# Twelve pairs of layer-1 row gathers made early and parked in DRAM, in a two-layer graph attention kernel

## The chip, the cores and the metric

The kernel runs on one core of a Trainium2 chip. The metric is the device time of one execution in microseconds (us). A core has five engines that run their own instruction streams: PE (TensorE, matmuls), DVE (VectorE), ACT (ScalarE), POOL (GpSimd) and SP (which only issues DMAs here). POOL also issues the indirect DMAs, which gather rows of a table by a list of row numbers.

## What is computed

A graph of N = 6250 nodes and E = 100000 edges, sorted by target, plus one own edge per node. Node features x are normalised, and then pass two graph attention layers and a small dense network:

```python
h = relu(layernorm(x))                        # (6250, 768)
# gat_conv(h, src, dst, W, a_src, a_dst, b, heads), with 4 heads in layer 1 and 1 head in layer 2:
h = (h @ W).reshape(n, heads, -1)             # 256 columns in all
alpha_s = (h * a_src).sum(-1); alpha_d = (h * a_dst).sum(-1)
e = leaky_relu(alpha_s[src] + alpha_d[dst], 0.2)
e = exp(e - segment_max(e, dst)[dst])
alpha = e / segment_sum(e, dst)[dst]
out = segment_sum(h[src] * alpha, dst) + b
# relu after each layer; then
out = x + relu(h @ Wm1 + bm1) @ Wm2 + bm2     # (6250, 768)
```

## The kernel before

All sizes go by 128 partitions. The nodes are NT = 49 tiles of 128, the edges 782 tiles of 128. Four edge tiles are a group (NG = 196 groups), two are a pair, and the work of four groups stands beside one node tile. Three stages follow one another.

**The feature stage** (loop over the 49 node tiles, after L386). SP loads a tile of x and its transpose. DVE takes the moments and subtracts the means (`centre`, L339), ACT applies relu (L341), PE multiplies by W1 in six fp32 products (`features1`, L350), and ACT writes the 256 results into the tile's row block in SBUF, `kept[i]` (`keep1`, L356), where each head has a column of ones beside its 64 columns. The eight scores of a node (source and target, four heads) are sums over products of its row with `a1`: POOL makes the products and adds halves (L365, L368), for the last four tiles DVE makes the products (L375), DVE adds the rest (L377), and ACT copies the four source scores to the end of the row (L378). `store1` (L381) then sends the row block to `table[1]` in DRAM.

**The edge stage of each layer** (`layer_edges`, L530) starts when the table is whole. POOL issues one indirect DMA for each edge tile (`gather`, L554), which brings the 128 source rows of 264 (layer 2: 258) numbers into one half of a pair buffer `G`. There are 20 pair buffers, and the gathers of group g + 8 are placed beside the work of group g (`AHEAD`). For each pair (`pair`, L612), ACT takes two exponentials of the source scores (L619, L621), DVE multiplies the second with the target's factor (L624), takes the maximum with the first (L634, in layer 2 L627), and weights the rows with it (L636; in layer 2 L631 puts the weight into the one-hot matrix instead). PE then adds the weighted rows to their targets, with a one-hot matrix of the targets ("hot", L582) as the other operand (L648). Masks for the target factors are made by DVE in layer 1 (L571), sent to DRAM, and read back in layer 2. When a node tile's sums are whole (`gather_up`, L659), its last steps are put on a list, and `advance` (L687) lets each of them go one step further, twice a group: `Node1.steps` (L796) divides, transposes, multiplies by W2, and stores the row block to `table[2]`, resting in between for a number of such half-groups (`rest`, L510). Layer 2's steps are the dense network and the output.

**Early gathers.** To bridge the wait for the last table rows, the first edge tiles of each layer are gathered before the table is whole (`EARLY`, L48). A row number that lies beyond the rows already stored is set to 0 and marked (`first_places`, L278); the missing rows are added later: DVE compares the source numbers with the numbers of the missing node tiles (`first_hits`, L258), PE multiplies the result with the `kept` tiles (`first_whole`, L273), and DVE joins both (L275). Layer 1 has 8 such gathers (L300): four once node tiles 0 to 43 are stored and four once 0 to 45 are. Layer 2 has 11: two behind tiles 0 to 45 and nine behind 0 to 46.

The order on each engine is the order in which the program is written; nothing reorders it. The engines wait for one another by semaphores.

Of the kernel before, what the change touches and what calls it, by code (L numbers as in the profile page):

```python
# [46 lines left out]

EARLY = {1: ((4, NT - 5), (4, NT - 3)), 2: ((2, NT - 3), (9, NT - 2))}  # L48
THERE = {layer: [there for n, there in stages for _ in range(n)] for layer, stages in EARLY.items()}

@with_exitstack
def kernel(
# [52 lines left out]

    iota_ps = ps.tile([P, P], F32, name="iota_ps", bufs=1)
    nc.vector.tensor_copy(iota_ps, iota)
    eps_c = const.tile([P, 1], F32, name="eps_c")  # L110
    nc.vector.memset(eps_c, EPS)
# [77 lines left out]
    def edge_places(ones):  # L189

        dst_i = ones.tile([P, NET], I32, name="dst_i")
        dri = ones.tile([NCH, CH], I32, name="dri")
        for to, of in ((dst_i, dst_cols), (dri, dst_rows), (src_i, src_cols)):
            nc.sync.dma_start(to, of)
            yield
            yield
        for layer in bT:
            with nc.allow_non_contiguous_dma(reason="256 numbers"):
                nc.sync.dma_start(bT[layer], {1: b1, 2: b2}[layer].rearrange("(k p) -> p k", p=P))
            yield  # L200
        b = ones.tile([P, OUT_DIM // P], F32, name="b")
        with nc.allow_non_contiguous_dma(reason="768 numbers"):
            nc.sync.dma_start(b, bm2.rearrange("(p k) -> p k", p=P))
        yield

        drm = ones.tile([NCH, CH], BF16, name="drm")
        nc.scalar.activation(dst_f, dst_i, AF.Copy)
        yield
        for d, to in ((dst_i, dcol), (dri, drm)):
            nc.vector.tensor_scalar(d, d, PAD_DST | P - 1, None, ALU.bitwise_and)  # L210
            yield
            nc.scalar.activation(to, d, AF.Copy)
            yield
        nc.sync.dma_start(dmod_d, drm)
        bp = ones.tile([P, 3, OUT_DIM // P], BF16, name="bp")
        rest = ones.tile([P, 2, OUT_DIM // P], F32, name="brest")
        in_parts(nc.vector, [bp[:, k] for k in range(3)], b, rest[:, 0], rest[:, 1])
        yield
        with nc.allow_non_contiguous_dma(reason="768 numbers"):
            nc.sync.dma_start(bm2_d.rearrange("s (p k) -> p s k", p=P), bp)  # L220
# [41 lines left out]
    def first_whole(pool, layer):  # L262

        j = 0
        for stage, (n, there) in enumerate(EARLY[layer]):
            if stage and layer == 1:
                first_hits(pool, layer, stage)
            for k in range(n):
# [23 lines left out]
    def first_rows(layer, stage):  # L292

        j = sum(n for n, _ in EARLY[layer][:stage])
        n, there = EARLY[layer][stage]
        for j in range(j, j + n):
            k, t = divmod(FIRST + j, 2)
            if k not in first_G[layer]:
                first_G[layer][k] = rows_in(layer)
            nc.gpsimd.indirect_dma_start(  # L300
                out=first_G[layer][k][:, t], out_offset=None, in_=table[layer][:there * P],
                in_offset=bass.IndirectOffsetOnAxis(ap=first_i[layer][:, j:j + 1], axis=0))
    mask_d = dram.tile([NU * P, 8 * P], BF16, name="mask_d")
    edges_stack.enter_context(tc.manual_schedule())
    with tc.tile_pool(name="w1p", bufs=1) as wp, tc.tile_pool(name="x1", bufs=6) as xp, \
# [38 lines left out]
        def features1(i):  # L344
            r, rstd = rs.pop(i)
            h_ps = ps.tile([P, HID], F32, name="h_ps", tag="o", bufs=3)
            for k in range(KI):
                if (i, k) == (1, 2):
                    spread_means(2)
                nc.tensor.matmul(h_ps, r[:, k], w1[:, k], start=(k == 0), stop=(k == KI - 1))  # L350
            return h_ps, rstd

        def keep1(i, h_ps, rstd):
            row = kept[i]
            h = heads_row(row)[:, :, :HID // 4]
            nc.scalar.activation(h, h_ps.rearrange("p (h c) -> p h c", h=4), AF.Copy, scale=rstd)  # L356

            ha = wk.tile([P, 8, HID // 4], F32, name="ha", bufs=2)
            four = ha.rearrange("p (k h) c -> p k h c", k=2)
            of = h.unsqueeze(1).to_broadcast([P, 2, 4, HID // 4])  # L360
            if i >= NT - 4:
                halves[i] = four, of
                return
            else:
                nc.gpsimd.tensor_tensor(four, of, a1b, ALU.mult)  # L365
                for n in (HID // 8, HID // 16):
                    hb = wk.tile([P, 8, n], F32, name=f"ha{n}", bufs=2 if n > 16 else 4)
                    nc.gpsimd.tensor_tensor(hb, ha[:, :, :n], ha[:, :, n:], ALU.add)  # L368
                    ha = hb
            halves[i] = ha  # L370

        def scores1(i):
            if i >= NT - 4:
                four, of = halves[i]
                nc.vector.tensor_tensor(four, of, a1b, ALU.mult)  # L375
                halves[i] = four.rearrange("p k h c -> p (k h) c")
            nc.vector.tensor_reduce(sd[1][:, i], halves.pop(i), AX.X, ALU.add)  # L377
# [18 lines left out]
        fetch_x(1)  # L396
        w1 = wp.tile([P, KI, HID], F32, name="w1")
        nc.sync.dma_start(w1, W1.rearrange("(k p) f -> p k f", p=P))
        fetch_xT(1)
# [5 lines left out]
        fetch_x(5)  # L405
        pieces = edge_places(ones)
        moments(0)
        spread_means(0)
# [5 lines left out]
        for i in range(NT):  # L414
# [23 lines left out]
            if i == 40:  # L438
                first_places()
            if i < NT - 5:  # L440
                keep1(i, *h)
                if i > 2:
                    store1(i - 3)
                if i > 1:
                    scores1(i - 2)
            else:
                for k in {NT - 3: (i - 2, i - 1)}.get(i, (i - 2,) if i < NT - 3 else (i - 1,)):
                    scores1(k)
                    if k == NT - 7:
                        store1(k - 1)  # L450
                    store1(k)
                keep1(i, *h)
            if i == NT - 6:
                first_sources(1)
            if i == NT - 4:
                first_rows(1, 0)
            elif i == NT - 2:
                first_rows(1, 1)
            if i >= 14:
                next(pieces, None)  # L460

        scores1(NT - 1)
        store1(NT - 1)

# [65 lines left out]
    def layer_edges(layer, H, node, pre, matched, pre_pool):  # L530
# [4 lines left out]
        with tc.tile_pool(name=f"eg{layer}", bufs=5) as eg, \  # L535
                tc.tile_pool(name=f"hw{layer}", bufs=10 if layer == 1 else 14) as hwp, \
                tc.tile_pool(name=f"sum{layer}", bufs=4) as sums, \
                tc.tile_pool(name=f"sm{layer}", bufs=4) as sm:
            G, hot, e_ps, o_ps = {}, {}, {}, {}

# [4 lines left out]
            def gather(g):  # L545
                if not 0 <= g < NG:
                    return
                for t in tiles(g):
                    k = TPG * g + t
                    if k // 2 not in G:  # L550
                        G[k // 2] = first_G[layer].get(k // 2) or rows_in(layer)
                    if k < FIRST + len(THERE[layer]):
                        continue
# [58 lines left out]
            def pair(g, p):  # L612
# [10 lines left out]
                rho, v, w = (e_ps[g // 4][:, at:at + 2, k * H:(k + 1) * H] for k in range(3, 6))  # L623
                nc.vector.tensor_mul(v, e2, rho)  # L624
                if layer == 2:
                    w = sm.tile([P, 2, H], F32, name="w")
                    nc.vector.tensor_max(w, v, e1)  # L627
                    hw = hwp.tile([P, 2, P], F32, name="hw")
# [4 lines left out]
                else:  # L633
                    nc.vector.tensor_max(w, v, e1)  # L634
                    hw = hwp.tile([P, 2, H, C + 1], F32, name="hw")
# [58 lines left out]
            if layer == 1:  # L694
                for r in range(4):
                    fetch_rows(r)
                first_whole(pre_pool, layer)
                for u in range(4):
# [9 lines left out]
            for g in range(NG):  # L708
# [14 lines left out]
                if j == 0:  # L723
                    if layer == 1:
                        fetch_rows(t + 4)
                    node.prefetch(t)
                    meet(t + 1)
                elif j == (2 if t < NT - 1 else 1):
                    node.ahead(t)
                elif j % 2:  # L730
                    make_mask((g + 7) // 2)
                if g == NG - 3:
# [12 lines left out]
                if NG - 3 <= g < NG - 1:  # L745
                    stay_warm(3)
                hot.pop(g, None)
                if layer == 1 and g == NG - 6:
# [24 lines left out]
    with tc.tile_pool(name="w2p", bufs=1) as wp, tc.tile_pool(name="wk2", bufs=2) as wk:  # L773
# [4 lines left out]
        class Node1:  # L778
# [17 lines left out]
            def steps(self, t, sum_, most=None, last=None):  # L796
# [12 lines left out]
                turn(o, p)  # L809
                yield from rest(7)  # L810
                rT = straighten(wk, 1, p)
                h_ps = ps.tile([P, HID + 2], F32, name="h_ps", tag="n")
                for k in range(KH):
                    nc.tensor.matmul(h_ps, rT[:, k], w2[:, k], start=(k == 0), stop=(k == KH - 1))
                yield from rest(7)
                row = kept[t][:, :TW[2]]
# [5 lines left out]
        with tc.tile_pool(name="pre1", bufs=1) as pre:  # L822
            first_hits(pre, 1, 0)
            pre1 = prepare(pre, 1, 4)
# [430 lines left out]
```

## Time and profile before

| | |
|---|---|
| median of 12 executions | 2148.82 us (2144.61 to 2150.55) |
| the profiled execution | 2148.88 us, of which the span from first to last instruction is 2147.0 us |
| mean granted TensorE clock | 0.828 of full |
| feature stage | about 0 to 155 us |
| gathers of layer 1 on POOL | 147.3 to 1135.6 us |
| gathers of layer 2 on POOL | 1141.3 to 2120.4 us |

The profile lists for each engine the time in which it ran instructions. A group of instructions is shown with its source line, engine, operation, output and inputs, the number of times, the summed time, the mean of one in ns, and the idle time of the engine just before it with what ended most of that. A row of the timeline has start, length, engine, line, operation and, in brackets, the idle time before it and what ended it; "issue" means that nothing the profile shows was waited for. Time in which an engine issues a plain DMA isn't counted as busy, but the indirect DMAs on POOL are.

### The profile page before, as it was taken

Reading aid. Unit: us, or ns where it says so; the run is one execution under the profiler, and the core shown is the slowest. Engines: PE = TensorE matmul, PEld = TensorE weight load, DVE = VectorE, ACT = ScalarE, POOL = GpSimd, SP = SyncE. Lnnn points to the kernel's source line nnn. Section 1 sums busy time; section 2 is a strip of 40 time slices with the busy share of each in tenths; the row PEclk is TensorE's granted clock in tenths of the full one; section 3 lists DMA queues with packets and bytes.
Section 4 is the critical chain, followed back from the end, with each engine's and each line's share of the span. In section 5 each row is a group of like instructions: output and inputs, shape, how many; then the busy total and the mean of one; then the engine's idle time right before and its main releaser. Section 6 shows DMA issues by size and latency. Waiting matters only on the chain.

```text
span 2147.0 us, 26518 instructions
## 1 busy us (share of the span) xinstructions
PE 1580.6 (74%) x6764; PEld 1087.1 (51%) x6765; DVE 1345.6 (63%) x4164; ACT 597.3 (28%) x2601; POOL 1602.6 (75%) x1759
## 2 busy tenths in 40 slices
PE   8997766666676666666668677777787787787777
PEld 6875444444444444444446454554554454454554
DVE  7887776667666667666666555555555555555554
ACT  4651222222222222222222222222222222222222
POOL 6877777777777777777776777777777777777773
PEclk9998878777777778777879888888878878888898
DMA  9966565555555555655556455556556556555553
GB/s 347 363 223 215 172 168 165 168 168 164 169 167 162 169 167 162 171 166 160 163 141 208 125 172 179 164 171 180 169 167 180 176 159 180 179 156 179 180 153 112
DMA packets 157543, 383.12 MB, mean 178 GB/s; under 512 B 35543, under 2 KB 50222, under 8 KB 157382
## 3 DMA queue, kind: packets, MB, share of 16 engines
q0 software_dynamic: 75072, 209.10, 36.5%
q1 hardware_dynamic: 80940, 170.75, 22.6%
q10 hardware_dynamic: 1370, 1.48, 0.3%
q8 instruction: 58, 0.95, 0.2%
q14 instruction: 103, 0.84, 0.1%
HBM read 323.07 MB, written 58.13 MB: 178 GB/s over the span
## 4 chain that ended last, share of the span: by engine, by line
DMA 32%; PE 26%; DVE 20%; issue 9%; POOL 6%; ACT 6%; ACTq 0%; DVEq 0%; POOLq 0%
DMA G<-table,src_i 32%; PE o_ps L648 11%; PE y_ps L939 7%; POOL G L554 6%; DVE hw L636 5%; PE h_ps L350 5%; DVE e_ps L624 2%; ACT e L619 2%; DVE hw L631 2%; DVE e_ps L634 2%; DVE hot L582 2%; ACT sum L678 2%; DVE acc L669 1%; PE y_ps L875 1%; PE tp L923 1%
## 5 line engine op out<-in xcount | busy, mean ns | idle before, releaser
L554 POOL DMA_INDIRECT G<-table,src_i x1545 | 1472.0, 953 | 470.7 <-issue 260.8
L648 PE MATMUL o_ps<-hw,hot 128*128 128x260 f32 x1564 | 576.9, 516 | 310.7 <-DVE hw L636 300.5
L648 PE MATMUL o_ps<-G,hw 128*128 128x258 f32 x1564 | 473.1, 439 | 227.4 <-DVE hw L631 227.0
L648 PEld LDWEIGHTS o_ps<-hw,hot 128*128 128x128 f32 x1564 | 362.3, 251 | 486.8 <-DVE hw L636 412.5
L624 DVE TENSOR_TENSOR e_ps<-e,e_ps 128x8 f32<-128x8 f32 (+1 forms) x782 | 129.7, 166 | 676.1 <-ACT e L621 667.9
L648 PEld LDWEIGHTS o_ps<-G,hw 128*128 128x128 f32 x1564 | 318.9, 217 | 355.1 <-DVE hw L631 294.2
L619 ACT ACTIVATE e<-G 128x8 f32<-128x8 f32 (+1 forms) x782 | 160.2, 205 | 1063.4 <-DMA G<-table,src_i 1022.6
L631 DVE TENSOR_SCALAR hw<-iota_ps,dcol,w 128x128 f32<-128x128 f32 x782 | 285.0, 406 | 14.4
L636 DVE TENSOR_TENSOR hw<-G,e_ps 128x520 f32<-128x520 f32 x391 | 271.8, 695 | 14.3 <-DVE e_ps L634 0.9
L678 ACT ACTIVATE sum<-acc 32x260 f32<-32x260 f32 (+1 forms) x384 | 160.0, 417 | 332.0 <-DVE acc L669 321.2
L939 PE MATMUL y_ps<-wm,mT 128*128 128x384 f32 x392 | 205.4, 660 | 0.7 <-ACT mT L928 0.7
L621 ACT ACTIVATE e<-G 128x8 f32<-128x8 f32 (+1 forms) x782 | 148.8, 190 | 0.7
L350 PE MATMUL h_ps<-w,r 128*128 128x256 f32 x588 | 135.2, 384 | 4.4 <-ACT r L341 4.4
L582 DVE TENSOR_TENSOR hot<-iota_ps,dcol 128x512 f32<-128x512 f32 x196 | 133.7, 682 | 0.0
L939 PEld LDWEIGHTS y_ps<-wm,mT 128*128 128x128 f32 x392 | 87.7, 248 | 66.2 <-issue 40.4
L350 PEld LDWEIGHTS h_ps<-w,r 128*128 128x128 f32 x588 | 109.7, 193 | 22.7 <-ACT r L341 5.7
L669 DVE SCALAR_TENSOR_TENSOR acc<-acc,keep,o_ps 128x260 f32<-128x260 f32 (+1 forms) x192 | 91.4, 476 | 0.4 <-PE o_ps L648 0.4
L634 DVE TENSOR_TENSOR e_ps<-e_ps,e 128x8 f32<-128x8 f32 x391 | 68.2, 174 | 13.4
L365 POOL TENSOR_TENSOR ha<-kept,a1b 128x512 f32<-128x512 f32 x45 | 53.2, 1183 | 26.9 <-ACT kept L356 26.8
L627 DVE TENSOR_TENSOR w<-e_ps,e 128x2 f32<-128x2 f32 x391 | 62.4, 159 | 13.3
L600 PEld LDWEIGHTS <-mask 128*128 128x128 bf16 x1564 | 57.3, 100 | 15.2 <-issue 8.3
L769 ACT ACTIVATE rT<-tp,bT 128x128 f32<-128x128 f32 x196 | 59.4, 352 | 7.1 <-PE tp L763 7.1
(405 smaller groups left out, 1124.2 us busy)
## 6 DMA issues: line engine op xcount, KB each, us to landing
xt<-in_x SPq DMA_DIRECT2D x96, 384.0 KB, 5.2
drow<-dmod_d SPq DMA_DIRECT2D x49, 512.0 KB, 5.2
mask_d<-mask SPq DMA_DIRECT2D x97, 256.0 KB, 2.5
mask<-mask_d SPq DMA_DIRECT2D x97, 256.0 KB, 5.0
G<-table,src_i POOLq DMA_INDIRECT x1545, 2.9
xTt<-in_xT SPq DMA_DIRECT2D x49, 384.0 KB, 5.8
out<-y SPq DMA_DIRECT2D x48, 384.0 KB, 2.3
table<-kept SPq DMA_DIRECT2D x49, 132.0 KB, 4.0
```

The costliest lines, as they stand in the source:

```text
L350: nc.tensor.matmul(h_ps, r[:, k], w1[:, k], start=(k == 0), stop=(k == KI - 1))
L554: nc.gpsimd.indirect_dma_start(out=G[k // 2][:, k % 2], out_offset=None, in_=table[layer], in_offset=bass.IndirectOffsetOnAxis(ap=src_i[:, ...
L582: nc.vector.tensor_tensor(hot[g][:, T[0]:T[0] + n], iota_ps.unsqueeze(1).to_broadcast([P, n, P]), dcol[:, k:k + n].unsqueeze(2).to_broadca ...
L619: nc.scalar.activation(e1, sc, AF.Exp)
L621: nc.scalar.activation(e2, sc, AF.Exp, scale=SLOPE)
L624: nc.vector.tensor_mul(v, e2, rho)
L631: nc.vector.tensor_scalar(hw[:, t], iota_ps, dcol[:, k:k + 1], w[:, t], ALU.is_equal, ALU.mult)
L636: nc.vector.tensor_mul(hw, Gp[:, :, :RW[1]].rearrange("p t (h c) -> p t h c", h=H), w.unsqueeze(3).to_broadcast([P, 2, H, C + 1]))
L648: nc.tensor.matmul(o_ps[u], l, r[:, :RW[layer]], start=(g % 2 == 0 and k == 0), stop=(g % 2 == 1 and k == tiles(g)[-1]))
L669: nc.vector.scalar_tensor_tensor(acc, run[0], keep[:, u % 2:u % 2 + 1], o_ps.pop(u), ALU.mult, ALU.add)
L678: nc.scalar.activation(done[t][r], acc[r], AF.Copy)
L939: nc.tensor.matmul(y_ps, mT[:, j], wm2[:, j, s * half:(s + 1) * half], start=False, stop=(j == KH - 1))
```

## The change

Layer 1 has no early gathers of its first tiles any more. In their place 24 gathers of 12 later pairs (pairs 23, 39, 55 and so on to 199, one in every two node tiles' work) are made near the end of the feature stage, each once the rows up to a given node tile are stored: four after 38 tiles, two each after 39 to 44, four after 45, two each after 46 and 47. Their rows go to DRAM (`soon_away`, on SP) and come back into a pair buffer when the gather of that pair would have been due (`soon_back`, on SP). The missing rows, of 11 to 2 node tiles, are made by DVE compares (`soon_hits`), PE products (`soon_missing`) and a DVE joining step (`soon_whole`), spread over the work of node tiles 0 to 24: each node tile has the work of one edge tile. The compares read the node numbers from PSUM (`nid_ps`).

The scores become eight more columns of W1 from node tile 8 on: POOL multiplies W1 with `a1` at the start, DVE sums into the weight columns, PE multiplies 264 columns in place of 256, and ACT copies the scores out of the result twice (to the row and to `sd`). Tiles 0 to 7 have their scores made as before, during tiles 8 to 15. From node tile 35 on a row block is stored in its own step of the loop.

In `pair`, the weighting of a pair's rows and the products with them (`onto_sums`) move behind the first weight operation of the next pair, save in the last two groups of a layer. Both rests of `Node1.steps` go from 7 to 4.

```diff
-EARLY = {1: ((4, NT - 5), (4, NT - 3)), 2: ((2, NT - 3), (9, NT - 2))}
+EARLY = {2: ((2, NT - 3), (9, NT - 2))}
...
+SOON = [NT - m for m in (11, 11, 10, 9, 8, 7, 6, 5, 4, 4, 3, 2)]
+SOON_AT = {2 * (8 * i + 11) + 1: i for i in range(len(SOON))}
+BARE = 8
...
+    def soon_rows(there):
+        for i in range(len(SOON)):
+            if SOON[i] == there:
+                soon_G[i] = rows_in(1)
+                for t in range(2):
+                    nc.gpsimd.indirect_dma_start(
+                        out=soon_G[i][:, t], out_offset=None, in_=table[1][:there * P],
+                        in_offset=bass.IndirectOffsetOnAxis(ap=soon_i[:, i, t:t + 1], axis=0))
+    def soon_away():
+        for i in range(len(SOON)):
+            nc.sync.dma_start(soon_d[i], soon_G.pop(i).rearrange("p t c -> p (t c)"))
+    def soon_back(i):
+        G = rows_in(1)
+        nc.sync.dma_start(G.rearrange("p t c -> p (t c)"), soon_d[i])
+        return G
...
+    def soon_hits(pool, k):
+        i, t = divmod(k, 2)
+        if i < len(SOON):
+            m = NT - SOON[i]
+            soon_hit[k] = pool.tile([P, NT - SOON[0], P], F32, name="soon_hit")
+            nc.vector.tensor_tensor(
+                soon_hit[k][:, :m],
+                soon_of[i][:, t * P:(t + 1) * P].unsqueeze(1).to_broadcast([P, m, P]),
+                nid_ps[:, SOON[i]:].unsqueeze(2).to_broadcast([P, m, P]), ALU.is_equal)
+    def soon_missing(k):
+        if 0 <= k < 2 * len(SOON):
+            there, hit = SOON[k // 2], soon_hit.pop(k)
+            soon_p[k] = ps.tile([P, TW[1]], F32, name="missing1", tag="n")
+            for T in range(there, NT):
+                nc.tensor.matmul(soon_p[k], hit[:, T - there], kept[T], start=(T == there),
+                                 stop=(T == NT - 1))
+    def soon_whole(G, k):
+        if 0 <= k < 2 * len(SOON):
+            i, t = divmod(k, 2)
+            row = G[soon_pair[i]][:, t]
+            nc.vector.scalar_tensor_tensor(row, row, soon_ok[:, i, t:t + 1], soon_p.pop(k),
+                                           ALU.mult, ALU.add)
...
-                nc.tensor.matmul(h_ps, r[:, k], w1[:, k], start=(k == 0), stop=(k == KI - 1))
+                nc.tensor.matmul(h_ps[:, :n], r[:, k], w1[:, k, :n], start=(k == 0), stop=(k == KI - 1))
...
+            if i >= BARE:
+                nc.scalar.activation(row[:, RW[1]:], h_ps[:, HID:HID + 4], AF.Copy, scale=rstd)
+                nc.scalar.activation(sd[1][:, i], h_ps[:, HID:], AF.Copy, scale=rstd)
...
+            if BARE < i <= SOON[0] - 3:
+                store1(i - 1)
+            if i >= SOON[0] - 3:
+                store1(i)
+                soon_rows(i + 1)
...
                 nc.vector.tensor_mul(v, e2, rho)
+                while weighed:
+                    onto_sums(*weighed.pop())
...
+                weighed.append((g, p, Gp, w))
+                if g >= NG - 2:
+                    onto_sums(*weighed.pop())
...
-                first_whole(pre_pool, layer)
+                soon_sources(pre_pool, 0)
+                soon_away()
+                fetch_rows(3)
...
+                    if layer == 1:
+                        soon_hits(pre_pool, t)
                 elif j % 2:
+                    if layer == 1 and j == 3:
+                        soon_missing(t)
+                    elif layer == 1:
+                        soon_whole(G, t - 1)
...
-                yield from rest(7)
+                yield from rest(4)
```

## The prediction

> **What bounds the kernel now.** I read the busy rows of the page first, then GpSimd (POOL) in order of time, because one group of its instructions, the row gathers, fills it.
>
> ```profile
> PE 1580.6 (74%) x6764; PEld 1087.1 (51%) x6765; DVE 1345.6 (63%) x4164; ACT 597.3 (28%) x2601; POOL 1602.6 (75%) x1759
> L554 POOL DMA_INDIRECT G<-table,src_i x1545 | 1472.0, 953 | 470.7 <-issue 260.8
> L648 PE MATMUL o_ps<-hw,hot 128*128 128x260 f32 x1564 | 576.9, 516 | 310.7 <-DVE hw L636 300.5
> L582 DVE TENSOR_TENSOR hot<-iota_ps,dcol 128x512 f32<-128x512 f32 x196 | 133.7, 682 | 0.0
> ```
>
> No engine looks full. But the 470.7 us of idle time over 1545 gathers is 0.305 us each, and the timeline of POOL shows what that is:
>
> ```profile
> 143.11 1.18 POOL L365 TENSOR_TENSOR ha<-kept,a1b 128x512 f32<-128x512 f32 x1 [0.18 <-ACT kept L356]
> ...
> 147.31 1.13 POOL L300 DMA_INDIRECT G<-table,first_i  x1 [1.67 <-DMA table<-kept]
> ...
> 158.49 1.01 POOL L554 DMA_INDIRECT G<-table,src_i  x1 [0.37 <-issue]
> ...
> 213.17 1.18 POOL L554 DMA_INDIRECT G<-table,src_i  x1 [0.30 <-issue]
> ...
> 1134.64 0.94 POOL L554 DMA_INDIRECT G<-table,src_i  x1 [0.30 <-issue]
> 1141.26 0.95 POOL L300 DMA_INDIRECT G<-table,first_i  x1 [5.67 <-DMA table<-kept]
> ...
> 1155.39 0.95 POOL L554 DMA_INDIRECT G<-table,src_i  x1 [0.30 <-DVE G L275]
> ```
>
> Every gather is followed by 0.30 us in which POOL starts the next one, whoever is named as releaser. One gather is thus 0.95 + 0.30 = 1.25 us of POOL, and it runs so without a break, but for the 5.67 us between the layers, from 147.3 us to the last gather at 2119.4 us. After that 26.6 us of tail remain (2147.0 - 2120.4). The 774 gathers of layer 1 took 1135.6 - 158.5 = 977.1 us (1.262 each), the 771 of layer 2 965.0 us (1.252 each). ACT waits 1022.6 us in all for gathered rows. So the time is: when the gathers begin, plus how many there are, plus the gap between the layers, plus the tail. POOL time saved in the edge layers comes off the end one for one, while the other engines have room. Do they? The table by stretches:
>
> ```profile
> 200.00:220.00 20.00, 12.65 (x57) 8.21 (x55) 16.29 (x45) 4.31 (x29) 15.12 (x17) 0.91 0.55 163
> 600.00:700.00 100.00, 69.69 (x270) 46.56 (x268) 67.42 (x187) 24.66 (x118) 76.09 (x79) 0.76 0.57 164
> ```
>
> The columns are length, PE, PEld, DVE, ACT, POOL, clock, DMA share, GB/s. In steady state PE and DVE are two thirds busy. From 181 to 222 us the consumers catch up on rows that are already there: by 222.4 us, 8 + (222.4 - 158.5) / 1.262 = 59 gathers (14.7 groups of four) had been issued, and all were consumed in 41.8 us. That is 2.8 us a group, 11.4 us a node tile (four groups), where POOL needs 16 x 1.26 = 20.2.
>
> **Gathers moved ahead.** Layer 1 loses its 8 early gathers and gets 24 (12 pairs of edge tiles). The stream behind them falls from 774 to 758: 16 x 1.25 = 20.0 us less, if it starts when it did. The 24 stand on POOL in front of the stream, each behind a table store: 24 x 1.3 (the 8 early ones of before averaged 1.40, beside DVE work that goes away) = 31 us. The row of node tile i is kept at ACT L356; I read 119.3 us for tile 37, 142.6 for 44, 148.0 for 46, 153.3 for 48. A store lands a median 4.0 us after issue. The first four gathers can go at 119.3 + 0.5 + 0.3 + 4.0 = 124 us, four at tile 44's landing (147), two each at 45's and 46's. By these the soon gathers end near 157 to 158 and tile 48's row has landed by 153.3 + 0.5 + 0.4 + 4.0 = 158: both limits fall where the stream starts today. POOL's score products, 45 x about 2.5 us, which filled it here until 145.6 us, are gone from tile 8 on, so it has the room.
>
> **Scores as columns.** Each feature tile on PE grows from 256 to 264 columns:
>
> ```profile
> 139.77 2.76 PE L350 MATMUL h_ps<-w,r 128*128 128x256 f32 x12
> ```
>
> 2.76 / 256 x 8 = 0.086 us, over 41 tiles 3.5 us. In the feature stage PE runs back to back but for the stalls on loads (4.7 us in two steps at 130 to 137 us, DMA nearly full until about 120 us), and a later PE fits into those: I take 1.5 us, with bounds 0 and 3.5. The second small ACT copy (0.20) fits: ACT has 1.8 us of work in a 2.70 us tile. POOL's six weight products (15 us from 12.5 us on) end before DVE's reductions of tiles 2 to 4 and before tile 8 needs them. So the stream begins at 158.5 + 1.5 = 160.0 us. That tile 48 no longer waits for a score product on DVE (0.69 + 0.69 us) is within this.
>
> **The missing rows and the way through DRAM.** 12 x 270 KB out and back on SP. The nearest row, a mask of 256 KB, lands in 5.0 us; reads are issued eight groups (40 us) ahead of use. The copies out stand behind three row fetches and hold 12 of the 20 pair buffers; the first is needed again by the 17th gather of the stream, 20 us after its start, by which time the first copies have gone. Nothing on POOL waits. The stores of tiles 35 to 48 now wait on SP for their own tile's row; behind them are loads needed five tiles (13 us) later. On PE the missing rows take 160 products of 128x264. Twelve such took
>
> ```profile
> 171.72 5.75 PE L273 MATMUL missing<-kept,hit 128*128 128x264 f32 x24 [0.98 <-DVE hit L258]
> ```
>
> 0.48 us each at a high clock; an edge product at the layer's clock of 0.77 takes 576.9 / 782 = 0.74. In the first four tiles, 10 or 11 products are 5.3 to 8.1 us, beside 13.2 us of PE work in a steady tile and a POOL pace that is now 15 gathers, 18.8 us. PE can thus fall 0 to 2.5 us behind per tile. The Trainium skill ("TensorE: Matmul & The Clock Gate", section "Part 1: The HAM clock gate") says that the clock comes back after about 3.4 us of sustained activity, which favours the lower end; the rows agree in kind (granted 1.00 in the full feature stage, 0.77 here). By either, the sum over all 24 tiles is at most 17 us, and POOL may run 20 pairs, 50 us, ahead before it waits for a buffer. I take 0. DVE gets 160 x 128 elements of compare, by the L582 row (682 / 512 = 1.33 ns) 27 us, and 24 corrections of 0.49 = 12 us, over 450 us: 68% becomes 77%.
>
> Here a rule speaks against the change. The skill ("GPSIMD Engine Reference", section "8. Key points") has GpSimd share its SBUF interfaces with VectorE, with contention when a DVE instruction has two SBUF inputs or runs in a two-port mode. The trace has both sides:
>
> ```profile
> 213.05 0.48 DVE L571 TENSOR_SCALAR mask<-drow,pidx 128x1024 bf16<-128x1024 bf16 x1
> 181.66 0.68 DVE L582 TENSOR_TENSOR hot<-iota_ps,dcol 128x512 f32<-128x512 f32 x1
> 181.56 0.95 POOL L554 DMA_INDIRECT G<-table,src_i  x1 [0.30 <-issue]
> ```
>
> The gather beside the mask took 1.18, the one beside the "hot" compare, which has one operand in PSUM, 0.95. The new compares also have one operand in PSUM (nid_ps), and so have the corrections. By the nearest row, "hot", they cost POOL 0; if they held it for all their length, 27 + 12 = 39 us.
>
> **One slot later, and the shorter rests.** The weighted rows of a pair now wait on DVE behind the next pair's first weight product, which waits for that pair's rows. PE gets them 2.5 us later, and a pair buffer comes free one pair of 20 later; while POOL bounds, 0. At the end of each layer the last two groups go at once, so the tail stays. Bounds -1 to +2. The rest counts fall from 7 to 4 half-groups. Counting the steps, tile 45's row of table 2 leaves one group earlier (group 193, not 194), tile 46's at 194 in both. At the gap between the layers two gathers need tiles up to 45, nine need 46. The two move into the 5.67 us gap: 2 x 1.25 = 2.5 us gained (bounds 0 and 5).
>
> **Sum.** -20.0 (16 gathers) + 1.5 (start) - 2.5 (gap) = -21.0 us. The profiled execution took 2148.88 us (span 2147.0 + 1.9), level with the median of 2148.82. 2148.8 - 21 = 2128 us.
>
> **The rivals.** Within 0.2% is 4.3 us, about what a measurement of this kernel tells from no change.
> - As summed, with its bounds: 2122 to 2134. POOL's unbroken row speaks for it. Chance 0.80.
> - The stream starts later. If the two ACT copies, or slower loads beside the early gathers, lengthen feature tiles by 0.2 us on the path (41 x 0.2 = 8.2), the time is 2136; half of the idle 0.35 us that DVE shows ahead of "cent" in each tile speaks against it. Chance 0.09.
> - PE becomes the bound in the first tiles and the buffers don't absorb it: 2128 + 17 = 2145. The catching up at 2.8 us a group speaks against it. Chance 0.05.
> - Slower: the 24 compares and 24 corrections of node tiles 0 to 24 hold GpSimd's gathers. Held throughout, 2128 + 39 = 2167; it ends above 2153 from 25 / 39, two thirds of their length, on. The mask held a gather 0.2 of its 0.48 us, "hot" not at all. Chance 0.06.
>
> Faster by over 0.2%: 0.89; within: 0.05; slower: 0.06. The range 2122 to 2139 takes in the first two cases.
>
> **What would show it.** Right: the first gather of table 1 near 125 us, the stream's first at 159 to 162, 1.25 us each with no idle time but 0.30, layer 1's last gather near 1117, the gap between the layers about 3 us. Wrong: gathers over 1.1 us beside the new compares; POOL waiting on DVE or PE for a buffer in the first 200 us of the layer; feature tiles above 2.8 us.

## The result and the profile after

The changed kernel takes 2127.83 us in the median (2126.13 to 2132.72, 7 executions) beside 2148.45 us for the kernel before: ratio 0.991, 95% interval 0.9901 to 0.9919. That is 20.6 us less. The prediction was 2128 us. The sum came out right, but two of its terms did not. They were off by about as much in opposite directions, so that the total fits this closely is luck.

The page of the profiled execution (2130.58 us, of which the span is 2128.8 us) has these rows of engines and of the layer-1 and layer-2 gathers:

```profile
PE 1617.6 (76%) x7020; PEld 1128.2 (53%) x7021; DVE 1276.1 (60%) x4178; ACT 601.2 (28%) x2642; POOL 1527.2 (72%) x1666
L621 POOL DMA_INDIRECT G<-table,src_i x1529 | 1456.3, 952 | 467.8 <-issue 266.3
```

Sixteen gathers have gone from the streams (1529 for 1545). PE was busy 37 us longer: the products for missing rows (L366) take 90.2 us, while the edge products of layer 1 (L723) took 36 us less than in the kernel before (540.7 for 576.9).

```profile
L723 PE MATMUL o_ps<-hw,hot 128*128 128x260 f32 x1564 | 540.7, 490 | 242.7 <-DVE hw L711 241.3
L366 PE MATMUL missing<-kept,soon_hit 128*128 128x264 f32 x320 | 90.2, 441 | 0.0
```

DVE was busy 69 us less, and this comes with the deferral of the weighted rows: DVE was busy 1264.6 us in the kernel before with the deferral alone, and 1355.7 us in the changed kernel without it (both runs follow). DVE has no less to do, for its rows add up to about the same before and after (1427 and 1437 us); its instructions overlap more. The timeline of POOL in the changed kernel gives the places where the time went (start, length, operation, idle time before it):

```profile
126.13 1.13 POOL L331 DMA_INDIRECT G<-table,soon_i  x1 [79.78 <-DMA xt<-in_x]
...
155.06 0.95 POOL L331 DMA_INDIRECT G<-table,soon_i  x1 [0.30 <-issue]
156.31 0.95 POOL L621 DMA_INDIRECT G<-table,src_i  x1 [0.30 <-issue]
...
1111.04 0.95 POOL L621 DMA_INDIRECT G<-table,src_i  x1 [0.30 <-issue]
1112.30 0.94 POOL L309 DMA_INDIRECT G<-table,first_i  x1 [0.30 <-issue]
...
1117.00 0.94 POOL L309 DMA_INDIRECT G<-table,first_i  x1 [2.51 <-DVE e_ps L696]
...
1130.63 0.94 POOL L621 DMA_INDIRECT G<-table,src_i  x1 [2.31 <-DVE G L284]
...
2095.47 0.95 POOL L621 DMA_INDIRECT G<-table,src_i  x1 [0.30 <-issue]
```

The 24 early gathers run from 126.1 us to 156.0 us at 1.25 us each, and the stream follows with no gap. Set beside the kernel before (its rows are in the prediction), the span divides so:

| stretch of the span | before | after | difference |
|---|---|---|---|
| to the start of layer 1's stream | 158.49 | 156.31 | -2.2 |
| layer 1's stream (774 and 758 gathers) | 977.1 | 955.7 | -21.4 |
| its end to the start of layer 2's stream | 19.8 | 18.6 | -1.2 |
| layer 2's stream (771 gathers) | 965.0 | 965.8 | +0.8 |
| last gather to the end | 26.6 | 32.4 | +5.7 |
| span | 2147.0 | 2128.8 | -18.2 |

The profiled execution lies 2.8 us above the median of the timed ones. The gap between the layers and the end vary by some 3 us from profile to profile, also among kernels that are alike there, so single differences in these two rows are rough.

The windows show that PE and DVE took the extra work beside the gathers (columns as in the prediction). The first row is the kernel before, the other three are the changed kernel:

```profile
260.00:400.00 140.00, 93.93 (x398) 65.30 (x398) 96.56 (x270) 34.53 (x168) 105.95 (x112) 0.79 0.60 170
200.00:220.00 20.00, 15.24 (x72) 11.76 (x71) 15.25 (x40) 3.91 (x20) 15.12 (x17) 0.84 0.61 174
260.00:400.00 140.00, 115.04 (x552) 90.31 (x551) 109.99 (x297) 35.31 (x181) 106.12 (x112) 0.88 0.64 183
600.00:700.00 100.00, 72.83 (x290) 48.55 (x290) 70.09 (x199) 24.75 (x125) 75.93 (x80) 0.78 0.61 173
```

POOL's busy time per microsecond (the fifth pair) is the same in all of them, while PE rises from 67% to 82% where the missing rows are made, and DVE from 69% to 79%.

### The profile page after: what moved, and what is told of

Same layout as the page of the kernel before. It is cut to its first block, busy times and chain, and to the rows that moved or that the text cites. A ratio compares the mean times of both kernels' runs of the same rounds, so it can differ in the third digit from the quotient of the medians.

```text
span 2128.8 us, 27330 instructions
## 1 busy us (share of the span) xinstructions
PE 1617.6 (76%) x7020; PEld 1128.2 (53%) x7021; DVE 1276.1 (60%) x4178; ACT 601.2 (28%) x2642; POOL 1527.2 (72%) x1666
## 4 chain that ended last, share of the span: by engine, by line
DMA 32%; PE 27%; DVE 21%; issue 9%; POOL 6%; ACT 5%; ACTq 0%; DVEq 0%; SPq 0%; POOLq 0%
DMA G<-table,src_i 30%; PE o_ps L723 11%; DVE hw L711 8%; PE y_ps L1023 6%; PE h_ps L424 6%; POOL G L621 6%; DVE e_ps L691 2%; ACT e L686 2%; ACT sum L753 2%; DVE e_ps L696 2%; DVE hw L707 2%; DVE acc L744 1%; DVE mask L638 1%; DVE hot L649 1%; ACT e L688 1%
## 5 line engine op out<-in xcount | busy, mean ns | idle before, releaser
L621 POOL DMA_INDIRECT G<-table,src_i x1529 | 1456.3, 952 | 467.8 <-issue 266.3
L723 PE MATMUL o_ps<-hw,hot 128*128 128x260 f32 x1564 | 540.7, 490 | 242.7 <-DVE hw L711 241.3
L723 PE MATMUL o_ps<-G,hw 128*128 128x258 f32 x1564 | 467.6, 436 | 233.4 <-DVE hw L707 233.0
L723 PEld LDWEIGHTS o_ps<-hw,hot 128*128 128x128 f32 x1564 | 340.9, 235 | 402.0 <-DVE hw L711 348.2
L723 PEld LDWEIGHTS o_ps<-G,hw 128*128 128x128 f32 x1564 | 316.5, 215 | 358.8 <-DVE hw L707 288.2
L424 PE MATMUL h_ps<-w,r 128*128 128x264 f32 (+1 forms) x588 | 136.1, 386 | 1.5 <-ACT r L414 1.4
L366 PE MATMUL missing<-kept,soon_hit 128*128 128x264 f32 x320 | 90.2, 441 | 0.0
L331 POOL DMA_INDIRECT G<-table,soon_i x24 | 22.9, 953 | 86.8 <-DMA xt<-in_x 79.8
L366 PEld LDWEIGHTS missing<-kept,soon_hit 128*128 128x128 f32 x320 | 73.5, 230 | 16.8
```

The source lines that it names most:

```text
L366: nc.tensor.matmul(soon_p[k], hit[:, T - there], kept[T], start=(T == there), stop=(T == NT - 1))
L424: nc.tensor.matmul(h_ps[:, :n], r[:, k], w1[:, k, :n], start=(k == 0), stop=(k == KI - 1))
L621: nc.gpsimd.indirect_dma_start(out=G[k // 2][:, k % 2], out_offset=None, in_=table[layer], in_offset=bass.IndirectOffsetOnAxis(ap=src_i[:, ...
L723: nc.tensor.matmul(o_ps[u], l, r[:, :RW[layer]], start=(g % 2 == 0 and k == 0), stop=(g % 2 == 1 and k == tiles(g)[-1]))
```

## The experiments

Every run is given with its ratio to the kernel before on the same chip and the 95% interval, since the kernel before itself took 2148.2 to 2152.7 us on the chips used.

**No deferral.** The weighted rows follow their own weight again.

```diff
-                if g >= NG - 2:
+                if g >= 0:
                     onto_sums(*weighed.pop())
```

> The changed kernel with a pair's weighted rows and products again straight behind its own weight, everywhere. Theory (the deferral lengthens the end of layer 2: the products of group 193's second pair stand on PE behind two steps of the dense network, and the sum of the last but one 64 targets waits for them): the time from the last gather to the end falls from 32.4 us back to about 26.6, the second wait of POOL between the layers (2.31 us) shrinks or goes, and the whole takes 2120 to 2123 us. Rival (the longer end is a chance of the granted clock, and the deferral costs nothing, as the prediction had it): 2127 to 2129 us, with an end above 30 us in this profile too or below it in both.

Measured: 2122.97 us, 0.9881 (0.9867 to 0.9895); 4.9 us less than the changed kernel. From the last gather to the end it took 27.3 us in place of 32.4. The reason is in the order of DVE and PE near the end. DVE in the kernel before, where the partial sum of the last but one stretch of 64 targets (`acc`) comes straight after the weights:

```profile
2120.88 0.73 DVE L631 TENSOR_SCALAR hw<-iota_ps,dcol,w 128x128 f32<-128x128 f32 x2
2121.53 0.48 DVE L669 SCALAR_TENSOR_TENSOR acc<-acc,keep,o_ps 128x258 f32<-128x258 f32 x1
```

PE and then DVE in the changed kernel:

```profile
2097.60 2.63 PE L1023 MATMUL y_ps<-wm,mT 128*128 128x384 f32 x4
2100.16 0.33 PE L959 MATMUL y_ps<-bm2r,ones_r 3*128 3x384 bf16 x1
2100.43 1.56 PE L1023 MATMUL y_ps<-wm,mT 128*128 128x384 f32 x4
...
2102.89 0.48 DVE L744 SCALAR_TENSOR_TENSOR acc<-acc,keep,o_ps 128x258 f32<-128x258 f32 x1 [3.68 <-PE o_ps L723]
```

DVE in this run:

```profile
2098.68 0.47 DVE L744 SCALAR_TENSOR_TENSOR acc<-acc,keep,o_ps 128x258 f32<-128x258 f32 x1
```

The last gather started at 2119.40 us before and at 2095.47 after. Counted from there, `acc` comes after 2.1 us and after 7.4 us. With the deferral the products of group 193's second pair stand on PE behind two halves of a dense layer (the `y_ps` rows, 4.8 us with their bias products). Without it, `acc` is at 2098.68 us, 2.8 us after the last gather's start at 2095.91. From `acc` to the end of the span it is 25.5 us before, 25.9 us in the changed kernel and 25.5 us in this run, so the later `acc` is nearly the whole of the longer end. POOL's second wait between the layers was 1.60 us for 2.31. Layer 1's stream (956.5 us) and layer 2's (964.9) are the same with and without deferral, within 1 us: the deferral does nothing for the steady stretch, as the prediction had it, and costs at the end, as it had not.

**Deferral up to group 192.** `NG - 3` in place of `NG - 2` in the same line.

> The changed kernel with the deferral kept up to group 192 and the immediate order from group 193 on (three last groups in place of two). Theory (only the second pair of group 193 matters): as without any deferral, an end of about 26.6 us and 2120 to 2123 us. If deferring costs or gives something in the steady stretch as well, this run and the one without any deferral differ by more than 1.5 us. Rival (deferral without effect): 2127 to 2129 us.

Measured: 2125.53 us, 0.9893 (0.9879 to 0.9908). The end took 26.9 us in the profile, so the deferral in group 193 is what lengthens it. The timed median is above the 2120 to 2123 us that I had named, and 2.6 us above that without any deferral, more than the 1.5 us named beforehand, but the intervals overlap. The profile has the difference between the layers: 20.1 us there, 17.8 without deferral. Whether deferral also costs there is not settled by these two runs.

**Only the deferral, in the kernel before.** The same lines of `pair`, nothing else.

> The kernel before with nothing but the deferral of a pair's weighted rows (as in the changed kernel, save in the last two groups of a layer). Theory (the deferral gives nothing while the gathers bound the layers, and costs 3 to 6 us at the end of layer 2): the last gather at 2120 us as before, an end of 29 to 32.5 us in place of 26.65, and 0.1 to 0.3% more than the kernel before (2150.5 to 2155 where that takes 2148.5). Rival (the deferral costs nothing): the ratio is 1.000.

Measured: 2151.67 us, 1.002 (1.0011 to 1.0029), 3.5 us slower than the kernel before. The end took 32.1 us for 26.65. In this profile POOL also waited 8.63 us between the layers (5.67 before); the span, 2157.5, lies well above the median, so only the end is read from it. By itself this part of the change is a loss.

The profiles of this document fall into two groups. In the seven with the deferral in group 193, `acc` comes 6.0 to 8.2 us after the start of the last gather, and the end takes 29.1 to 32.4 us (30.5 in the mean). In the six without it, `acc` comes 2.1 to 3.3 us after, and the end takes 25.6 to 28.5 us (27.1). The changed kernel's 32.4 us is the longest of all; the difference of the means is 3.4 us.

**Marking of early rows spread out, in the kernel before.** The prediction put the feature stage's last stalls down to loads. The timeline of the kernel before has this on DVE and PE, in feature tile 40 and after:

```profile
127.96 1.18 DVE L284 TENSOR_SCALAR first_ok<-src_i 128x9 f32<-128x9 int32 x1
...
132.57 4.54 PE L350 MATMUL h_ps<-w,r 128*128 128x256 f32 x12 [2.42 <-ACT r L341]
```

All eight marking instructions (L284, L285) stand together in front of the next tile's moments; then PE waits, and its next products take 4.54 us in place of 2.76. This kernel gives them out two to a tile:

```diff
+                yield                      # in first_places, after each of its four stages
...
-            if i == 40:
-                first_places()
+            if i == 33:
+                places = first_places()
+            if i >= 33:
+                next(places, None)
```

> The kernel before, with its eight small DVE instructions that mark early row numbers (all in feature tile 40) given out two to each of the feature tiles 33 to 36. Theory (the 4.7 us that the feature stage lost at 127 to 137 us came from these instructions standing in front of the next tile's moments and means on DVE, and from the lower clock of PE after the idle time): the first early gather starts 4 to 5 us sooner, at 142 to 143.5 us, and the whole takes 2143.5 to 2145 us. Rival (the stall came from the loads, as the prediction had it): the stall stays, 2148 to 2149 us.

Measured: 2145.1 us, 0.9985 (0.9976 to 0.9993). PE now runs through from 125 to 139 us with 2.76 us a tile, and the first early gather starts 5.7 us sooner:

```profile
141.63 1.13 POOL L301 DMA_INDIRECT G<-table,first_i  x1 [1.67 <-DMA table<-kept]
```

So the burst of small DVE instructions was the cause. Of the 5.7 us, 3.4 arrive in the median and 1.7 in the profile. There layer 1's stream took 979.0 us for 977.1, the gap between the layers 20.7 for 19.8, and the end 27.6 for 26.65; why is open.

**Node numbers read from SBUF.** `nid` in place of `nid_ps` in the compares for missing rows, so that they have two SBUF operands.

> The changed kernel with the node numbers of the 24 compares read from SBUF in place of PSUM, so that a compare has two SBUF operands. Theory (two SBUF operands hold GpSimd, for about the 0.2 of 0.48 us that the mask holds it, and one does not): gathers beside the compares take up to 1.5 us, 27 us of compares cost POOL 11 us (27 if held throughout), and the whole takes 2137 to 2155 us. Rival (the compares do not hold GpSimd in either form): 2127 to 2129 us.

Measured: 2135.22 us, 0.9936 (0.9923 to 0.9948), 7.4 us slower than the changed kernel. The compare and the gather beside it in this kernel, DVE and then POOL:

```profile
196.09 1.62 DVE L356 TENSOR_TENSOR soon_hit<-soon_of,nid 128x1408 f32<-128x1408 int32 x1
196.45 2.08 POOL L621 DMA_INDIRECT G<-table,src_i  x1 [0.30 <-issue]
```

and in the changed kernel, with the numbers in PSUM:

```profile
215.71 1.61 DVE L356 TENSOR_TENSOR soon_hit<-soon_of,iota_ps 128x1408 f32<-128x1408 int32 x1
215.64 0.96 POOL L621 DMA_INDIRECT G<-table,src_i  x1 [0.30 <-issue]
```

The compare is as long in both; the gather is 2.08 us beside the one and 0.96 beside the other. Layer 1's stream took 963.2 us for 955.7, all 24 compares being some 25 us (24 of about 1.0 us): 7.5 us, or 30% of their length. I had named 11 us and at least 2137 us, which was too much. The rule of the Trainium skill ("GPSIMD Engine Reference", section "8. Key points") that spoke against the change agrees with this run, where a compare has two SBUF operands, and the change keeps clear of it by one operand in PSUM.

**Six pairs.** `SOON` with (6, 5, 4, 4, 3, 2) only.

> The changed kernel with 6 early pairs in place of 12 (behind 43 to 47 stored node tiles, at places 23 to 103 in the order of the pairs): 12 gathers more in the stream of layer 1, and 48 in place of 160 products for missing rows. Theory (each gather that is moved ahead of the stream is worth 1.25 us, and the extra work on PE and DVE costs nothing): the stream starts within 2 us of 156.3 us, and the whole takes 2127.8 + 12 x 1.25 = 2142.8 us (2141 to 2145). Rival (the missing rows cost time in the first tiles): less than 15 us worse, 2131 to 2140 us.

Measured: 2144.59 us, 0.9966 (0.9954 to 0.9978), on a chip where the kernel before took 2152.65. Against the kernel before it gains 8.1 us, where twelve pairs gain 20.6: 12.5 us for 12 gathers, 1.04 us each. The stream starts sooner with six pairs (152.98 us), because POOL has fewer gathers to finish before it; that gives back 3.3 us. I had named a start within 2 us of the changed kernel's 156.3.

**No early pairs.** `SOON` empty; scores as columns, deferral and short rests stay.

> The changed kernel without any early gather of layer 1 (scores as columns, deferral and shorter rests stay): all 782 gathers stand in the stream. Theory (the gain is the early gathers', 1.25 us each, and the rest of the change gives only a start that is a little sooner): POOL begins when tile 48's row has landed, at 153 to 155 us, layer 1's last gather is near 1140 us, and the whole takes 24 x 1.25 = 30 us less the 2 us of sooner start more than the changed kernel, 1.003 of the kernel before (2153 to 2157 where that takes 2148.5). Rival (the columns and the deferral make the layer faster by themselves): at or below the kernel before.

Measured: 2156.05 us, 1.0041 (1.0028 to 1.0055), slower than the kernel before, which had 8 early gathers. POOL starts its gathers only near the end of the feature stage:

```profile
154.84 1.13 POOL L621 DMA_INDIRECT G<-table,src_i  x1 [108.52 <-DMA w<-in_W]
```

Against the kernel before: 0 pairs +7.9 us, 6 pairs -8.1, 12 pairs -20.6. That is 28.5 us for 24 gathers, 1.19 each, a little less than the 1.25 us of POOL that each takes; the stream of the changed kernel starts 1.5 us later than this one. (The wait is put down to a load of `w`, which SP issues just behind the store of tile 48's row. The packets of that store end at 153.1 us, 1.8 us before the stream starts; in the kernel before it is 1.4 us. So I take the wait to be for that row.)

This kernel lacks the 8 early gathers of the kernel before, too. At 1.25 us each, an estimate, these are 10 us, so the rest of the change gains about 2 us: in the profile a start 3.7 us sooner and a gap 2.4 us shorter, against an end 3.6 us longer. So the change's 20.6 us are 28.5 for the 24 gathers and about 2 for the rest, less the 10 for the 8 gathers that went. No run has the score columns alone, so their share is not shown.

**Products twice.** Each sum of missing rows is made on PE twice; the second overwrites the first.

> The changed kernel with each sum of missing rows made twice on PE (the second overwrites the first), 320 products in place of 160, so up to 22 more matrix products in the work of one node tile. Theory (the 20 pair buffers let POOL run ahead while PE is behind): POOL shows no wait for a buffer and the whole stays at 2127 to 2130 us. Rival (PE is at the edge of bounding the first tiles): 80 more us of products on PE show as waits of POOL, and the whole takes 2135 to 2160 us.

Measured: 2130.64 us, 0.9904 (0.9889 to 0.992), on the chip where the kernel before took 2152.65: no difference from the changed kernel. A window of this run, and POOL's longest entry of waits from 155 to 700 us (total, times, longest):

```profile
260.00:400.00 140.00, 125.38 (x657) 103.26 (x655) 111.01 (x297) 30.83 (x180) 106.15 (x112) 0.99 0.63 182
POOL G L621 <- issue: 78.3, 257, 0.3
```

No wait of POOL in the layer is longer than 0.3 us. The products for missing rows took 154.9 us in place of 90.2, but the edge products of layer 1 took 31 us less (509.6 for 540.7), so PE was busy only 30.5 us longer. In the window it is 90% busy, at a granted clock of 0.99 in place of 0.88 (and 0.79 in the kernel before). What PE would do with these products at a lower clock is not shown.

**Rests of 7.** Both rests of the node steps back at 7.

> The changed kernel with both rests of layer 1's node steps back at 7 half-groups. Theory (the row of node tile 45 leaves a group earlier by the shorter rests and lets two gathers of layer 2 into the gap between the layers): the two gathers stand behind the wait again, which is 5 us in one piece; but what follows them waited 2.3 us for tile 48's row in the changed kernel and need not wait any more, so that the gain of 2.5 us is mostly taken back by that second wait: 2127.5 to 2130 us. Rival (the shorter rests carry the whole 2.5 us): 2130 to 2131 us; or the longer rests hold up PE through the PSUM buffers that the missing rows share: above 2133 us.

Measured: 2134.07 us, 0.9919 (0.9905 to 0.9932), on the chip where the kernel before took 2152.65. The gain is 18.6 us against 20.6. The intervals of the two ratios overlap; the profile has the one wait in place of two:

```profile
1121.89 0.95 POOL L309 DMA_INDIRECT G<-table,first_i  x1 [7.00 <-DVE e_ps L691]
```

From the end of layer 1's stream to the start of layer 2's it took 21.2 us for 18.6. So the shorter rests are worth 2 to 3 us, what the prediction took, and not less as I expected here.

**Sixteen pairs, no deferral.** `SOON` begins with 15, 14, 13, 12; the rest as it was.

> 16 early pairs in place of 12, behind 34 to 47 stored node tiles (missing rows of 15 to 2 node tiles, 274 products), and no deferral. Theory (1.25 us for each gather that leaves the stream, the missing rows hidden): 8 gathers fewer than the run with 12 pairs and no deferral, 2123.0 - 10 = 2113 us (2111.5 to 2115.5). Rival (16 of the 20 pair buffers are held at the start of the layer, so that the stream waits for the copies to DRAM, or PE falls behind by more than the buffers hold): 2117 us or more, with waits of POOL in the first 100 us of the layer.

Measured: 2121.78 us, 0.9857 (0.9842 to 0.9872), on the chip where the kernel before took 2152.65. Against twelve pairs without deferral this is 5.3 us for 8 gathers in place of 10. No wait of POOL inside the layer shows; what is missing is at the start:

```profile
130.91 0.94 POOL L331 DMA_INDIRECT G<-table,soon_i  x1 [4.06 <-DVE cent L412]
...
161.08 0.95 POOL L621 DMA_INDIRECT G<-table,src_i  x1 [0.30 <-issue]
```

POOL stood idle for rows not yet stored, 5.3 us in two pieces, and then ran its early gathers until 161 us. The packets of the store of tile 48's row end at 154.1 us, so by the 1.4 us of the kernel before (157.1 us to the stream's start at 158.49) the stream could have begun at 155.5, an estimate. The rival's number came true, but not its reason: the copies and PE did not hold the stream.

**Sixteen pairs, two each behind the first tiles.** (15, 15, 14, 14, 13, 12, 11, 10, 9, 8, 7, 6, 5, 4, 3, 2), no deferral.

> 16 early pairs without deferral, with two pairs each behind the 34th and 35th stored node tile, so that POOL finds work while it waited (5.3 us in the run with 16 pairs) for the next rows. Theory (POOL's own queue of early gathers now sets when the stream starts): the stream starts at 156.5 to 158 us in place of 161.1, and the whole takes 0.9825 to 0.9845 of the kernel before, against 0.9857. Rival (products of missing rows, now 290, or the copies hold the layer): no better than 0.9857.

Measured: 2115.03 us, 0.9847 (0.9834 to 0.9861). The stream starts as expected:

```profile
156.98 0.95 POOL L621 DMA_INDIRECT G<-table,src_i  x1 [0.30 <-issue]
```

The ratio is 0.0002 above what I had named and overlaps with that of the other order, so by time alone the two cannot be told apart. Against twelve pairs without deferral it gains 7.6 us for 8 gathers. It is the fastest version measured: 33.2 us below the kernel before and faster than the changed kernel (0.991) by more than both intervals.

## Why the prediction was right, and where its terms were not

**Bound by gathers.** Right. The 16 gathers less were put at 20.0 us; layer 1's stream is 21.4 us shorter, and every version's stream but that with two SBUF operands (1.27) is its number of gathers times 1.26 us: 782 took 986.3 us, 770 took 972.1, 758 took 955.7.

**Start of the stream.** The step "In the feature stage PE runs back to back but for the stalls on loads" failed. The stall at 130 to 137 us came from the marking instructions of early rows on DVE and from the low clock after it (granted 0.83 from 130 to 140 us, 1.00 from 120 to 130), for both went in the spread version. The change cut these to the four of layer 2 in that place, and layer 1's come two pairs at a time in tiles 20 to 25. The wider products cost what was put down (12 took 2.84 us for 2.76, 3.3 us over 41 tiles), but the stall went. The last tile's products end at 150.3 us for 153.2, and without the score steps on DVE its row is whole at 151.0 for 155.4. The stream starts at 156.3 us, not 160.0, and what sets it is no longer that row but POOL itself: 24 gathers of 1.25 us from 126.1 us on end at 156. The store's packets end at 153.4 us, so the row would have allowed 154.8 (the same estimate with 1.4 us).

**The missing rows and DRAM.** Right at 0: no wait of POOL above 0.3 us inside the layer even with twice the products. By its own row of 600 to 700 us, a steady tile has 14.1 us of PE work (69.7% of 20.2), not 13.2, so the bound should have been 3.4 us per tile in place of 2.5. It was not reached: up to 400 us the missing rows took 58.1 us for 112 products, 0.52 us each, near the lower figure of 0.48, at a granted clock of 0.84 in that stretch.

**Compares beside the gathers.** Right at 0, and by the row that was named ("hot"). The rival had a real mechanism: with both operands in SBUF it costs 7.4 us. That is 30% of the compares' length, so even then it would not have carried the change to the slower side.

**Gap between the layers.** The mechanism was right (two gathers moved ahead). The two profiles of the table give -1.2 us for the -2.5, but over all profiles the size is right too: the gap is 17.3 to 20.5 us in the nine with rests of 4 (18.7 in the mean) and 19.8 to 22.5 us in the four with rests of 7 (21.1). What was late next, and not looked for, is tile 48's row: POOL's second wait of 2.31 us in front of layer 2's stream ends 1.5 us after the last packets of that row's store.

**Deferral.** The step "At the end of each layer the last two groups go at once, so the tail stays" failed. I looked at when a pair's rows are weighted, and not at what is put between on PE: the pair deferred out of group 193 is overtaken by the dense layer's products. It measured +5.7 us in the profile of the changed kernel, 3.4 us in the mean of all profiles, 4.9 us by the run without deferral, and 3.5 us in the kernel before.

So of the median's -20.6, the sum of the runs is about -25.6 without the deferral and +4.9 for it. The number held because the start was judged 3.7 us too late and the end 3.4 to 5.7 us too early. These slips lie in different stages, and that they cancel is luck; without the deferral the same sum would have been about 5 us off.

## What to carry to other kernels

Where one queue is full from end to end, work taken out of it is worth its own length, and the check on any extra work elsewhere is only whether the queue ever waits; look at the waits of that queue, not at the other engines' shares. An edit that delays a step by a slot is harmless where the queue bounds, but at the end of the stream everything is latency: write out the order on each engine for the last groups, and ask what now stands in front of the last sums. When a stall is to be used as cover, find its cause first; the change may remove it.

## What the runs showed of the hardware

A compare with two SBUF operands lengthened the gather beside it from 0.96 to 2.08 us; the same compare with one operand in PSUM did not. TensorE's granted clock was higher in the kernels that gave it more products in the window from 260 to 400 us: 0.79, 0.88 and 0.99 with 398, 552 and 657 matmul instructions (before, changed, products twice). It is no fixed relation: with rests of 7 it was 0.89 with 464. Nor is the busy time its measure: with no early pairs PE was busy 101.6 us there, more than the 93.9 of the kernel before, with fewer instructions (375) and a clock of 0.72. Doubling the products for missing rows cost nothing that the time shows.
